# Six fp32 weight products of a two-layer graph network by Strassen's algorithm, in three phases of two weights

**Chip, cores, metric.** One core of one Trainium2 chip. The metric is the device time in microseconds (us) of one execution, taken on the chip; a "tile" is 128 tokens (two graphs of 64 nodes) on the partitions, a "pair" is two tiles, and there are 64 tiles.

## The reference

Everything is fp32. Cut to what matters:

```python
x: (128, 64, 768)   adj: (128, 64, 64) bool, symmetric, with the diagonal
# layer 0: 12 heads of 64
h    = einsum('bnd,ade->bane', x, W)                  # product 1, weight W
th   = tanh(h)
attn = th @ w_src + swap(th @ w_dst)                  # one number per node and head
attn = leaky_relu(attn, 0.2); attn = where(~adj, -999, attn)
f    = elu(softmax(attn) @ h + b)                     # mixing, 64 x 64 per graph and head
gate = sigmoid(x @ H_w.T + H_b)                       # product 2, weight H_w
x    = layernorm(x + gate * f + (1 - gate) * x)
# layer 1: 6 heads of 128
q, k, v = x @ Wq + bq, x @ Wk + bk, x @ Wv + bv       # products 3, 4, 5
p    = softmax(q @ k.T / sqrt(128) + where(adj, 0, -9e15))
x    = layernorm(x + (p @ v) @ Wf + bf)               # product 6
```

## The kernel before

All six weights lie in SBUF. A unit of layer 0 (half the heads of one tile) and the pieces of layer 1 for an earlier group of two tiles alternate in one stream, so that layer 0's work on VectorE, GpSimd and ScalarE lies beside the products of both layers. The parts that the change and the argument touch:

```python
def product(lhsT, w, half):                    # W, H_w, Wv, Wf: 128 tokens x 384 columns
    ps = psm.tile([P, HALF], F32, name="pm")
    for c in range(NC):                        # six matmuls of 128x384
        nc.tensor.matmul(ps, lhsT[:, c, :], w[:, c, halves(half)], start=(c == 0), stop=(c == NC - 1))
    return ps
...
for w, bias, name in ((wq_sb, bq_c, "qT"), (wk_sb, bk_c, "kT")):     # q, k: 256 tokens at a time
    for c in range(NC):
        nc.tensor.matmul(ps, w[:, c, cols], x1T[:, c, :, :], start=(c == 0), stop=(c == NC - 1))
...
def softmax(s, n):
    nc.vector.tensor_reduce(mx[:, :n], s, AX.X, ALU.max)
    nc.vector.tensor_tensor(s, s, mx[...].to_broadcast(...), ALU.subtract)
    nc.scalar.activation(s, s, AF.Exp)
    nc.vector.tensor_reduce(sm[:, :n], s, AX.X, ALU.add)
    nc.vector.reciprocal(rs[:, :n], sm[:, :n])
    nc.gpsimd.tensor_tensor(s, s, rs[...].to_broadcast(...), ALU.mult)
...
pieces = [(5, scores, (hd,)) for hd in range(HEADS)] + ...   # layer 1's pieces, each with its weight
# ---- the units of layer 0 in turn, each a step behind in parts, between pieces of layer 1 ----
```

## Time and profile before

| | before |
|---|---|
| time, median of 3 runs | 3660.8 us (3659.2 to 3661.57) |
| TensorE busy, instructions | 99%, 16228 |
| VectorE, GpSimd, ScalarE busy | 47%, 23%, 22% |
| mean granted clock of TensorE | 0.997 |

```profile
DVE  4545444544444454444544454444445444454442
```

### The profile page before, as it was taken

How to read it: one execution, taken by the hardware profiler on the slowest of the kernel's cores; microseconds unless marked ns; L12 is line 12 of the kernel's file. 1: busy time of each engine (PE TensorE's matmuls, PEld its weight loads, DVE VectorE, ACT ScalarE, POOL GpSimd, SP SyncE). 2: the span in 40 equal slices, each digit the busy share in tenths (PEclk: the TensorE clock that was granted, in tenths of full speed). 3: DMA queues.
4: the chain of work that ended last, by engine and by line, in shares of the span. 5: the costliest groups of instructions: out<-in, count | busy, mean ns of one | idle time of the engine just before them, and what ended most of it. 6: DMA issues, size and time to landing. Idle time of an engine off the chain costs nothing.

```text
span 3657.3 us, 40929 instructions
## 1 busy us (share of the span) xinstructions
PE 3605.6 (99%) x16228; PEld 2544.3 (70%) x16228; DVE 1721.5 (47%) x3821; ACT 810.4 (22%) x1925; POOL 852.3 (23%) x904
## 2 busy tenths in 40 slices
PE   6999999999999999999999999999999999999999
PEld 4776677766777666777667776677766677766776
DVE  4545444544444454444544454444445444454442
ACT  2222222222222222222222222222222222222221
POOL 2222212222222222122222222222222222222120
PEclk9999999999999999999999999999999999999999
DMA  6000000000000000000000000000000000000000
GB/s 204 1 18 18 18 10 9 18 18 18 9 10 18 18 18 10 9 18 18 18 18 9 9 18 18 18 9 10 18 18 18 9 10 18 18 18 14 5 5 18
DMA packets 44031, 69.25 MB, mean 19 GB/s; under 512 B 23104, under 2 KB 23104, under 8 KB 43840
## 3 DMA queue, kind: packets, MB, share of 16 engines
q1 hardware_dynamic: 43840, 66.64, 5.3%
q8 instruction: 128, 2.10, 0.2%
q14 instruction: 63, 0.52, 0.0%
HBM read 41.46 MB, written 25.17 MB: 18 GB/s over the span
## 4 chain that ended last, share of the span: by engine, by line
PE 88%; DVE 9%; POOL 1%; ACT 1%; SPq 0%; issue 0%; DMA 0%; POOLq 0%; ACTq 0%
PE pm L177 47%; PE pm L345 28%; PE pa L303 3%; PE pa L280 3%; PE pa L379 2%; PE pa L355 2%; PE pa L202 1%; DVE st L214 1%; POOL s L284 1%; DVE x L396 1%; PE pa L170 1%; DVE z L323 1%; DVE s L287 1%; DVE x L324 1%; DVE mx L185 1%; DVE s L283 1%
## 5 line engine op out<-in xcount | busy, mean ns | idle before, releaser
L345 PE MATMUL pm<-x1T,wq_sb 128*128 128x256 f32 x2304 | 560.3, 384 | 0.3 <-DVE x1T L171 0.3
L177 PE MATMUL pm<-w_sb,xT 128*128 128x384 f32 x1536 | 534.3, 494 | 13.9 <-DVE xT L171 13.4
L345 PE MATMUL pm<-x1T,wk_sb 128*128 128x256 f32 x2304 | 528.6, 379 | 0.0
L177 PE MATMUL pm<-wv_sb,x1T 128*128 128x384 f32 x1536 | 519.8, 488 | 0.0
L177 PE MATMUL pm<-wf_sb,cT 128*128 128x384 f32 x1536 | 517.9, 487 | 0.4 <-DVE cT L388 0.4
L177 PE MATMUL pm<-hw_sb,xT 128*128 128x384 f32 x1536 | 516.3, 486 | 0.0
L345 PEld LDWEIGHTS pm<-x1T,wk_sb 128*128 128x128 f32 x2304 | 437.8, 190 | 59.5
L345 PEld LDWEIGHTS pm<-x1T,wq_sb 128*128 128x128 f32 x2304 | 424.9, 190 | 62.6 <-DVE x1T L171 0.6
L177 PEld LDWEIGHTS pm<-hw_sb,xT 128*128 128x128 f32 x1536 | 291.8, 190 | 203.5
L177 PEld LDWEIGHTS pm<-w_sb,xT 128*128 128x128 f32 x1536 | 284.6, 190 | 199.8 <-DVE xT L171 21.1
L177 PEld LDWEIGHTS pm<-wf_sb,cT 128*128 128x128 f32 x1536 | 286.9, 190 | 187.3 <-DVE cT L388 0.7
L177 PEld LDWEIGHTS pm<-wv_sb,x1T 128*128 128x128 f32 x1536 | 284.3, 190 | 173.4
L358 DVE SCALAR_TENSOR_TENSOR s<-pa,fill 128x128 f32<-128x128 f32 x192 | 54.9, 286 | 661.7 <-PE pa L355 661.7
L250 POOL TENSOR_TENSOR tmp<-th,ws_bc 128x384 f32<-128x384 f32 x128 | 127.6, 997 | 903.7 <-ACT th L248 872.8
L194 POOL TENSOR_TENSOR s<-s,rs 128x384 f32<-128x384 f32 x192 | 177.2, 930 | 666.3 <-DVE rs L193 666.3
L284 POOL TENSOR_TENSOR s<-s,adjf 128x384 f32<-128x384 f32 x128 | 127.7, 998 | 717.1 <-DVE s L283 717.1
L209 ACT COPY pt<-pa 64x192 f32<-64x192 f32 x637 | 199.6, 313 | 428.0 <-PE pa L202 407.3
L303 PEld LDWEIGHTS pa<-h,pt 128*128 128x128 f32 x1536 | 195.4, 194 | 35.3 <-ACT pt L209 1.2
L246 DVE COPY h<-pm 128x384 f32<-128x384 f32 x128 | 71.3, 557 | 285.1 <-PE pm L177 285.1
L248 ACT ACTIVATE th<-pm 128x384 f32<-128x384 f32 x128 | 62.9, 491 | 592.6 <-DVE h L246 592.6
L303 PE MATMUL pa<-h,pt 128*128 128x64 f32 x1536 | 189.1, 273 | 0.1
L316 ACT ACTIVATE tmp<-tmp 128x384 f32<-128x384 f32 x128 | 66.9, 523 | 474.4 <-DVE tmp L315 474.4
(65 smaller groups left out, 3482.8 us busy)
## 6 DMA issues: line engine op xcount, KB each, us to landing
x<-in_x_dram SPq DMA_DIRECT2D x64, 384.0 KB, 2.9
out_dram<-x SPq DMA_DIRECT2D x64, 384.0 KB, 2.3
w_sb<-in_L_gnn_W_dram SPq DMA_DIRECT2D x6, 384.0 KB, 6.3
x<-in_L_gnn_H_w_dram SPq DMA_DIRECT2D x6, 384.0 KB, 7.2
wq_sb<-in_L_gnn_Wq_dram SPq DMA_DIRECT2D x6, 384.0 KB, 6.4
wk_sb<-in_L_gnn_Wk_dram SPq DMA_DIRECT2D x6, 384.0 KB, 7.8
wv_sb<-in_L_gnn_Wv_dram SPq DMA_DIRECT2D x6, 384.0 KB, 7.8
wf_sb<-in_L_gnn_Wf_dram SPq DMA_DIRECT2D x6, 384.0 KB, 7.8
```

Source lines behind the costliest of these rows:

```text
L177: nc.tensor.matmul(ps, lhsT[:, c, :], w[:, c, halves(half)], start=(c == 0), stop=(c == NC - 1))
L194: nc.gpsimd.tensor_tensor(s, s, rs[:, :n, None].to_broadcast([P, n, S]), ALU.mult)
L209: nc.any.tensor_copy(pt_v[own, :, h2, own], ps[h2 * S : (h2 + 1) * S, :, own])
L246: nc.vector.tensor_copy(h, ph)
L250: nc.gpsimd.tensor_tensor(tmp, th, ws_bc[:, hs], ALU.mult)
L280: nc.tensor.matmul(pd, same_graph, dg, start=True, stop=True)
L284: nc.gpsimd.tensor_tensor(s, s, adjf[:, i, None, :].to_broadcast([P, AH, S]), ALU.mult)
L303: nc.tensor.matmul(po[:, a, :], pts[0][:, a, :], h[:, a * E : (a + 1) * E], start=True, stop=True)
L316: nc.scalar.activation(e, e, AF.Exp)
L345: nc.tensor.matmul(ps, w[:, c, cols], x1T[:, c, :, :], start=(c == 0), stop=(c == NC - 1))
L355: nc.tensor.matmul(pc[own, i, :], qk[0][:, i, own], qk[1][:, i, own], start=True, stop=True)
L379: nc.tensor.matmul(pc[:, j, :], vs[i][:, hd * P : (hd + 1) * P], pts[1][:, hd, :], start=True, stop=True,)
```

## The change

The intent: TensorE is full, so take an eighth of its dense work away. Each product of two 2 x 2 block matrices needs 7 block products instead of 8 (Strassen's algorithm, in Winograd's form with few sums). The sums of the operands are formed by VectorE and GpSimd; the sums of the results are formed in PSUM, by reading an accumulator between two products that add to it. Seven combinations of a weight take 7/4 of its room; the changed kernel holds two weights at a time: phase 1 does W and H_w (layer 0) for all tiles in pairs, phase 2 does Wq and Wk on groups of eight tiles, phase 3 does Wv and Wf in pairs. Between the phases x1 (plain and transposed) and the probabilities go through DRAM. The diff, condensed to its core (lines joined and shortened; `...` marks what is left out):

```diff
+def block_products(mm, done):                 # 7 products in 3 PSUM accumulators A, B, D
+    s0: mm(A, P1, True)
+    s1: mm(B, P6, True);   done("p1", A)
+    s2: mm(D, P7, True);   done("r", B)       # r = B + P1, read before the next line adds to B
+    s3: mm(B, P5, False);  done("w", B)       # w = B + P1, again a read between two additions
+    s4: mm(A, P2, False);  done("c11", A); done("c22", D)
+    s5: mm(B, P3, False);  done("c12", B)
+    s6: mm(D, P4, False);  done("c21", D)
+def token_major(comb, w):                     # W, H_w, Wv, Wf: three matmuls of 128x384 a product
+    for c in range(CH):
+        nc.tensor.matmul(ps[:, :HALF], comb[i][:, c, :], w[:, i, c, :],
+            start=start and c == 0, stop=c == CH - 1, skip_group_check=not start)
-            xTs[t] = work.tile([P, NC, P], F32, name="xT")
-            transposed(xs[t], xTs[t])
+            nc.vector.tensor_sub(c[P7], c[P1], a21); nc.vector.tensor_add(c[P5], a21, c[P4])
+            nc.gpsimd.tensor_tensor(c[P6], c[P4], c[P7], ALU.subtract)
+            nc.gpsimd.tensor_tensor(c[P3], c[P2], c[P6], ALU.subtract)
 ...                                          # phase 1, step p of 33: 14 products of pair p, and
+            dense = h_pieces(p) + g_pieces(p)  # ahead of the numbered ones:
+            add(side, 9 + 2 * i, scores, 2 * p + i)        # pair p
+            add(side, 12, prep, p + 1)
+            add(side, 2 * i, spread, t, 0)                 # t: the tiles of pair p - 1
+            add(side, 2 * i + 1, probs, t)                 # leaky, mask, softmax
+            add(side, 5 + 3 * i, turned, t, 0)             # transposes of the probabilities
+            add(side, 7 + 3 * i, mixed, t, 0)
+            add(side, 8 + 3 * i, rest, t)                  # elu, gate, residual, layernorm
+            add(side, 14, x1_turned, t)                    # transposed result, to DRAM
 ...
+x1_d, x1T_d, pr_d = DRAM tiles                # phase 1 -> 2 and 3, 1 -> 2 and 3, 2 -> 3
```

Layer 0's operations now take all 12 heads at once (768 columns), and the mask is one addition of 0 or -1e30 instead of a product and a sum.

## The prediction

Its 0.4292 us for a 512-column instruction lies on the straight line through the two spacings that it measures (0.2158 us for 256 columns, 0.3225 for 384). Its 0.557 us for a VectorE operation of 384 columns is in its trace (L246). The 6 us that bring its second rival to 50 us a pair are an estimate that no run had shown.

> **What bounds the kernel now.** I read the page's busy shares and slices first, then the chain that ended last, then the groups of instructions, then TensorE and VectorE instruction by instruction in the timeline.
>
> ```profile
> PE 3605.6 (99%) x16228; PEld 2544.3 (70%) x16228; DVE 1721.5 (47%) x3821; ACT 810.4 (22%) x1925; POOL 852.3 (23%) x904
> ...
> PE   6999999999999999999999999999999999999999
> ...
> PE 88%; DVE 9%; POOL 1%; ACT 1%; SPq 0%; issue 0%; DMA 0%; POOLq 0%; ACTq 0%
> ```
>
> TensorE is full in every slice but the first, and 88% of the chain is TensorE. No other engine passes half. So the time is TensorE's instruction stream plus the start. What the stream consists of, from the groups:
>
> ```profile
> L345 PE MATMUL pm<-x1T,wq_sb 128*128 128x256 f32 x2304 | 560.3, 384 | 0.3 <-DVE x1T L171 0.3
> L177 PE MATMUL pm<-w_sb,xT 128*128 128x384 f32 x1536 | 534.3, 494 | 13.9 <-DVE xT L171 13.4
> ```
>
> There are two groups of the first kind (q, k) and four of the second. The mean of one (384, 494 ns) is not its price, as matmuls overlap. The price is the distance between starts in the timeline:
>
> ```profile
> 1822.99 2.75 PE L345 MATMUL pm<-x1T,wk_sb 128*128 128x256 f32 x12
> 1825.58 1.03 PE L345 MATMUL pm<-x1T,wq_sb 128*128 128x256 f32 x4
> ...
> 1889.63 4.03 PE L177 MATMUL pm<-w_sb,xT 128*128 128x384 f32 x12
> 1893.50 4.03 PE L177 MATMUL pm<-hw_sb,xT 128*128 128x384 f32 x12
> ```
>
> Twelve 384-column instructions take 1893.50 - 1889.63 = 3.87 us, 0.3225 each; twelve 256-column ones 2.59 us, 0.2158 each. Each fp32 matmul of the source is two such instructions (64 tiles x 12 products = 768, and the row says 1536). The six products are then 6144 x 0.3225 + 4608 x 0.2158 = 1981 + 994 = 2976 us. In the same way from the timeline, the small work: 1536 mixing matmuls (L303) at 0.107, 768 of L379 at 0.115, 1344 transposes at 0.109, 1536 of L355 at 0.048, 256 of L280 at 0.3225: 165 + 88 + 147 + 74 + 83 = 557 us. Together 3533 us. The rest of 3657 is the start (first product at 27.9 us), an end of some 8 us, and about 90 us lost where kinds alternate.
>
> [...] So I estimate 512 columns at 429.2 ns. [...] one such line lasts 0.558 us at the median and up to 1.236:
>
> ```profile
> L324 DVE SCALAR_TENSOR_TENSOR x<-x,z x128: 545/558/1236, 56.5 to 3560.0; 128x384 f32<-128x384 f32 x128
> ```
>
> **The change, part by part.**
>
> *Removed from TensorE.* Strassen takes 7 block products for 8. For a pair of tiles and one of the four token-major weights it is 7 x 3 = 21 matmuls for 24; for q and k, on groups of eight tiles, 63 of 512 columns per weight for 144 of 256. So 5376 instructions x 0.3225 = 1734 us, and 2 x 8 x 63 x 2 = 2016 x 0.4292 = 865 us. Sum 2599, a saving of 377 us. The counts of small matmuls stay. TensorE's own work becomes 3533 - 377 = 3156 us: per pair of tiles in phase 1, 84 x 0.3225 = 27.1 plus 11.7 small = 38.8 us; phase 2, 865 + 74 = 939 us in all; phase 3, 30.5 us per pair.
>
> *Added elsewhere.* Three accumulators serve a block of seven products, and TensorE waits twice per block for a read of the bank it will add to next (first r, then w, from the same bank), and once for c22. Each read has one product's time to happen: 3 x 2 x 0.3225 = 1.94 us, or 2.58 us in phase 2. In a free VectorE (0.56 us, 0.69 for 512 columns) it is hidden.
>
> *VectorE in phase 1.* From the instruction order of the changed kernel, per pair: 27 ops of 384 columns (operand sums 2, h 5, gate 8, spread 4, mixed 4, statistics 4) and 20 of 768 (four reductions for the scores, eight in the softmaxes and leaky part, eight in the residual), plus 1.5 us of small ones: 27 x 0.557 + 20 x 0.96 + 1.5 = 35.7 us beside 38.8 of TensorE. Back to back they start closer than they last:
>
> ```profile
> 1851.11 0.55 DVE L186 TENSOR_TENSOR s<-s,mx 128x384 f32<-128x384 f32 x1
> 1851.58 0.55 DVE L317 SCALAR_TENSOR_TENSOR z<-z,tmp 128x384 f32<-128x384 f32 x1
> 1852.05 0.22 DVE L228 TENSOR_SCALAR fill<-adjf 128x128 f32<-128x128 f32 x1
> ```
>
> 0.47 us apart instead of 0.56. So VectorE's load is some 33 us, yet in strict order with waits for GpSimd and ScalarE between. GpSimd's own load per pair is about 21 us, by these prices, doubled for 768 columns:
>
> ```profile
> L250 POOL TENSOR_TENSOR tmp<-th,ws_bc 128x384 f32<-128x384 f32 x128 | 127.6, 997 | 903.7 <-ACT th L248 872.8
> ...
> L365 POOL TENSOR_TENSOR x<-x,bf_bc 128x768 f32<-128x768 f32 x64 | 115.0, 1820 | 100.3 <-PE pa L170 100.3
> ```
>
> I then walked one pair by hand[...], in us from the first product of h, at 1.94 a product and the durations above. (1) r of h is read at 4.7; the spreads and the leaky part of the first tile end at 7.6; GpSimd adds its mask until 9.5; VectorE, in order, takes the max at 9.6, a spread, the subtraction and the second tile's leaky part, and so reads w at 13.0 to 13.6, when TensorE wanted that bank at 12.9: stall 0.8. (2) The first tile's sum follows exp at 14.5, its reciprocal stands behind the second tile's max, which waits for GpSimd until 15.0, so GpSimd divides from 16.2 to 18.1 and TensorE's transposes of the probabilities, wanted at 15.6, start at 18.2: stall 2.5. (3) r of the gate stands behind a score reduction that waits for GpSimd's product until 30.0: read at 32.5, wanted at 31.1: 1.5. (4) c22 of the gate stands behind the second tile's statistics and the wait for GpSimd's power: read at 42.5, wanted at 41.0: 1.5. (5) The turn of the second tile's result waits for its layernorm: 1.9. That is 8.2 us, 47 us per pair. The shorter distances of some 40 ops give back about 3. I take **44 us** a pair.
>
> *The three phases.* Start 25 us to the first product and 29 us for a first pair without side work; 31 x 44 = 1364; then a tail with no dense work, one latency chain of softmax, mixing, residual, layernorm and turn, with the second tile behind it: 36. Into phase 2: both weights are issued before the end, but three of the four operand loads stand behind the last store, 0.8 MB each, then three sums of 1536 columns at 1.76: 18. Phase 2: 939 and some 11 for stalls behind the softmaxes: 950. Into phase 3: weights come during k, the first pair's transposed rows must be loaded and summed on GpSimd: 10. Phase 3: 32 x 31 with alternation = 992, stalls of 0.7 a pair: 1015. End: layernorm and store, 10. Sum 25 + 29 + 1364 + 36 + 18 + 950 + 10 + 1015 + 10 = 3457, say **3460 us**. So of the 377 us, 200 arrive; roughly 160 go to stalls in phase 1 and the rest to the two hand-ons.
>
> **The rivals.** *TensorE stays the bound everywhere.* The code spreads its side work over the fourteen products, which speaks for it, as does VectorE's 47% before. Then a phase-1 pair costs about 40 us: 3457 - 31 x 4 = 3333. *VectorE becomes phase 1's bound[...].* [...] Then 50 us a pair: 3643, no gain. The single line above that stretched was hit in few of its 128 cases, which speaks against the full size. *DRAM traffic and small packets hold it up.* The page has 19 GB/s before; the change adds 25 MB six times over (x1 out and in, its transpose out and twice in, the probabilities out and in at half that each), 151 MB in 3.4 ms or 44 GB/s, while the first slice moved 204 GB/s. That is hidden except at the hand-ons; if those cost 60 us more, 3520. *The products stall in all phases* (each read a little late): 14 more stalls of 0.3 us in 32 pairs of phase 3 would be 130 us, 3590; VectorE is only some 12 us of 31 there, which speaks against it.
>
> **Range and chances.** The pair of phase 1 is the wide term: 41 to 48 us give 3364 to 3581; the hand-ons add 20 either way. I take 3350 to 3600. Faster than 3588 with 0.85, within 2% 0.12, slower 0.03.
>
> **What would show it right or wrong.** Right: 5376 matmuls of 128x384 at 0.32 us apart and 2016 of 128x512 at 0.43; TensorE idle in phase 1 put down to VectorE and GpSimd (accumulator reads, probabilities, turns) at about 5 us a pair; phase 1 ending near 1455 us; VectorE's busy digits at 7 or 8 in phase 1, 4 in phase 2 and 3 or 4 in phase 3; gaps of 50 and 10 us at the hand-ons. Wrong: a phase-1 period below 41 (the walk too pessimistic) or over 48[...]; a stretched 512-column instruction; phases 2 or 3 more than 3% over their TensorE work.

## The result, and the profile after

The changed kernel takes **3538.6 us** (median of 4 runs, 3536.2 to 3541.5), before 3660.2 us in the same rounds: ratio **0.967**, 95% interval 0.965 to 0.968. A ratio here is the mean time of one kernel's fast runs over that of the other's of the same rounds, so not quite the ratio of the medians.

The page of the kernel after: busy shares, slices, chain.

```profile
PE 3280.1 (93%) x12868; PEld 1935.3 (55%) x12868; DVE 1830.0 (52%) x3067; ACT 852.3 (24%) x1677; POOL 1287.8 (36%) x984
...
PE   8888988889889888859999999999899999999998
...
DVE  4777777777777777752444234433433333333333
...
PE 46%; DVE 25%; POOL 18%; ACT 5%; issue 4%; SPq 0%; DMA 0%; POOLq 0%; ACTq 0%; DVEq 0%
```

TensorE's busy time fell by 325 us and the span by 118. The slices show three phases: up to the 17th, VectorE stands at 7 and TensorE at 8 or 9; in the rest TensorE is full. And the chain of waits, which was 88% TensorE, is now only 46%. The same by stretch (columns: stretch, length, then busy us of TensorE, weight loads, VectorE, ScalarE and GpSimd, granted clock, DMA share, GB/s):

```profile
50.00:1450.00 1400.00, 1246.15 (x5235) 811.28 (x5234) 1008.59 (x1657) 528.86 (x1040) 655.68 (x416) 0.96 0.16 50
...
1560.00:2480.00 920.00, 909.00 (x3449) 420.02 (x3450) 339.57 (x439) 85.80 (x128) 42.83 (x30) 0.99 0.12 41
...
2560.00:3500.00 940.00, 919.67 (x3418) 576.17 (x3417) 335.41 (x750) 176.71 (x390) 455.27 (x444) 1.00 0.27 85
```

Phases 2 and 3 are TensorE-bound, as predicted. In phase 1 TensorE is idle 11% of the time. The instructions of TensorE in one pair of phase 1 (from the timeline; the wait before an instruction and what ended it stand in brackets):

```profile
818.27 2.17 PE L180 MATMUL pm<-w,comb 128*128 128x384 f32 x6 [0.25 <-DVE w L350]
822.98 0.87 PE L220 MATMUL pa<-ident,s 128*128 128x128 f32 x6 [2.54 <-POOL s L214]
...
838.18 3.43 PE L180 MATMUL pm<-w,comb 128*128 128x384 f32 x6 [2.02 <-DVE r L376]
841.40 1.94 PE L442 MATMUL pa<-h,pt 128*128 128x64 f32 x12
843.18 2.15 PE L180 MATMUL pm<-w,comb 128*128 128x384 f32 x6
...
855.61 0.88 PE L477 MATMUL pa<-ident,z 128*128 128x128 f32 x6 [0.49 <-ACT z L202]
```

L220 are the transposes of the probabilities, waiting for GpSimd's division; L180 with "r" is a product that waits for VectorE's read of the accumulator. After the second wait six products take 841.40 - 838.18 = 3.22 us instead of 1.94, because the granted clock was halved for a while (columns as in the table by stretch above):

```profile
839.02:842.43 3.41, 3.41 (x11) 2.20 (x9) 3.41 (x4) 0.00 (x0) 2.05 (x1) 0.50 0.00 0
842.43:869.74 27.31, 24.12 (x94) 14.59 (x93) 21.50 (x40) 10.27 (x16) 9.91 (x7) 1.00 0.27 87
```

The clock records of the trace have 27 such stretches of 3.41 us at half clock from 100 to 1400 us, one a pair, so a pair loses about 1.7 us of TensorE time to them. They do not follow every wait: after the first one above, at 823, the clock stayed at 1.00. The mean pair, from the starts of GpSimd's L403 between 200 and 1300 us (all "pair" figures below are taken so), takes 46.95 us, and TensorE waits 143 us in the 1300 us from 100 to 1400, which is 5.2 us a pair.

The hand-ons, on TensorE's timeline: the tail of phase 1 has two waits of over 10 us, phase 2 begins at 1566.67, and phase 3 waits for its first transposed rows from DRAM.

```profile
1523.29 1.54 PE L477 MATMUL pa<-ident,z 128*128 128x128 f32 x6 [10.80 <-ACT z L202]
...
1539.76 1.54 PE L220 MATMUL pa<-ident,s 128*128 128x128 f32 x6 [10.46 <-POOL s L214]
...
1566.67 4.13 PE L572 MATMUL pm<-a,w 128*128 128x512 f32 x6
...
2515.64 4.21 PE L180 MATMUL pm<-w,xT 128*128 128x384 f32 x6 [11.16 <-DMA xT<-x1T]
```

### The profile page after: what moved, and what is told of

Same layout as the page of the kernel before. It is cut to its first block, busy times and chain, and to the rows that moved or that the text cites. A ratio compares the mean times of both kernels' runs of the same rounds, so it can differ in the third digit from the quotient of the medians.

```text
span 3539.0 us, 34181 instructions
## 1 busy us (share of the span) xinstructions
PE 3280.1 (93%) x12868; PEld 1935.3 (55%) x12868; DVE 1830.0 (52%) x3067; ACT 852.3 (24%) x1677; POOL 1287.8 (36%) x984
## 4 chain that ended last, share of the span: by engine, by line
PE 46%; DVE 25%; POOL 18%; ACT 5%; issue 4%; SPq 0%; DMA 0%; POOLq 0%; ACTq 0%; DVEq 0%
PE pm L572 25%; PE pm L180 16%; POOL u L396 5%; POOL s L427 3%; ACT pt L227 3%; DVE st L194 3%; DVE z L463 2%; DVE z L458 2%; POOL s L214 2%; POOL rstd L199 2%; DVE mx L207 2%; DVE sd L397 2%; DVE s L426 2%; DVE z L459 2%; DVE z L462 2%
## 5 line engine op out<-in xcount | busy, mean ns | idle before, releaser
L180 PE MATMUL pm<-w,comb 128*128 128x384 f32 x2688 | 981.9, 510 | 50.8 <-DVE r L376 34.3
L180 PEld LDWEIGHTS pm<-w,comb 128*128 128x128 f32 x2688 | 511.3, 199 | 375.0 <-issue 64.5
L572 PE MATMUL pm<-o,w 128*128 128x512 f32 x1152 | 524.0, 598 | 0.0
L572 PE MATMUL pm<-a,w 128*128 128x512 f32 x864 | 389.2, 595 | 7.2 <-issue 7.2
L572 PEld LDWEIGHTS pm<-o,w 128*128 128x128 f32 x1152 | 215.8, 190 | 258.3 <-issue 254.1
L180 PE MATMUL pm<-w,so 128*128 128x384 f32 x768 | 271.7, 497 | 25.8 <-DVE r L723 20.3
L572 PEld LDWEIGHTS pm<-a,w 128*128 128x128 f32 x864 | 164.8, 191 | 214.5 <-issue 214.5
L180 PE MATMUL pm<-w,sc 128*128 128x384 f32 x768 | 263.6, 486 | 0.0
L180 PE MATMUL pm<-w,xT 128*128 128x384 f32 x576 | 203.7, 490 | 11.2 <-DMA xT<-x1T 11.2
L180 PEld LDWEIGHTS pm<-w,so 128*128 128x128 f32 x768 | 143.0, 193 | 121.0 <-DVE r L723 27.5
L180 PE MATMUL pm<-w,cT 128*128 128x384 f32 x576 | 201.3, 486 | 0.0
L180 PEld LDWEIGHTS pm<-w,sc 128*128 128x128 f32 x768 | 141.1, 190 | 85.6 <-DVE r L777 0.6
L403 POOL TENSOR_TENSOR dg<-eye,sd 128x768 f32<-128x768 f32 x64 | 113.5, 1773 | 131.5 <-DVE sd L397 130.3
```

The costliest lines, as they stand in the source:

```text
L180: nc.tensor.matmul(ps[:, :HALF], comb[i][:, c, :], w[:, i, c, :], start=start and c == 0, stop=c == CH - 1, skip_group_check=not start,)
L403: nc.gpsimd.tensor_tensor(dg, eye[:, None, :].to_broadcast([P, A, S]), sd[:, 1, :, None].to_broadcast([P, A, S]), ALU.mult,)
L572: nc.tensor.matmul(ps, w[:, i, c, j * P : (j + 1) * P], opers[g][i][:, c, :], start=start and c == 0, stop=c == CH - 1, skip_group_check=n ...
```

## The experiments

The question: 377 us of TensorE work were taken away and 122 us arrived. Where did the rest go, and what sets phase 1? Theory A was that the streams of VectorE and GpSimd set the pair and TensorE merely waits for them; its rivals were (B) that TensorE's own work counts in full with waits on top, and (C) that each wait comes from one instruction's place in its engine's stream and can be moved away. Each expectation says itself what its theories mean (B means something else in nomax_udve, and D comes in with nomax_split); 46.85 and 45.7 us in them are earlier readings of the pairs of the changed kernel and of nomax. All twelve kernels but the last give correct results, and a ratio is to the kernel before (3661 us) in the same rounds.

| run | us | ratio | pair, us | TensorE waits a pair, us | lost to the clock a pair, us |
|---|---|---|---|---|---|
| changed kernel | 3538.6 | 0.967 | 46.95 | 5.2 | 1.7 |
| plain_p1 | 3677.3 | 1.005 | 51.96 | 5.8 | 2.3 |
| plain_all | 3865.1 | 1.056 | 51.75 | 5.8 | 2.4 |
| repeat | 3616.3 | 0.988 | 49.42 | 5.9 | 1.7 |
| nomax | 3505.2 | 0.958 | 46.08 | 4.6 | 1.7 |
| defer | 3558.6 | 0.972 | 47.75 | 5.7 | 1.6 |
| turn | 3520.2 | 0.962 | 46.32 | 4.3 | 1.7 |
| turn_scores | 3559.8 | 0.973 | 47.83 | 4.5 | 3.4 |
| turn_scores_nomax | 3549.0 | 0.970 | 47.78 | 4.7 | 3.4 |
| nomax_split | 3503.1 | 0.957 | 46.08 | 4.6 | 1.7 |
| nomax_udve | 3516.3 | 0.961 | 46.75 | 5.1 | 2.3 |
| nomax_behind | 3516.6 | 0.960 | 46.90 | 5.0 | 2.3 |
| cut (wrong result) | 3523.2 | 0.962 | 47.06 | 4.9 | 2.6 |

The last but one column is the sum of TensorE's waits from 100 to 1400 us, times the pair, over 1300. It stays between 4.3 and 5.9. The last is half of the time for which the trace's clock records show half clock, brought to a pair in the same way. A pair is TensorE's own work (38.8 us; 42.7 in the plain kernels, 40.7 in repeat), plus these two, plus 0.5 to 1.7 us of the rest. This split adds up by construction and names no cause.

### What the phases cost, and what Strassen gives

The same three phases with the ordinary eight block products, first in phase 1 alone, then everywhere:

```diff
-        w_w = weight(load_w)                 # seven combinations
+        w_w = weight_plain(load_w)           # four blocks
-            return block_products(token_major(combs[p], w_w), done)
+            return block_plain(token_plain(combs[p], w_w), done)   # c11 = P1 P1 + P2 P2, and so on
```

> Phase 1 with plain block products (8 for 7), phases 2 and 3 left with Strassen. Theory A: a pair of phase 1 (46.85 us) is set by VectorE and GpSimd taking turns in order, and TensorE only waits; then 3.87 us more TensorE work per pair cost nothing, and the 7 VectorE and 2 GpSimd operations that go make the pair shorter: 44 to 45 us (TensorE's own 42.7 plus alternation is the floor), some 3470 us in all. Theory B: TensorE's work plus stalls that have other causes sets it: 46.85 + 3.87 = 50.7 us a pair, 3660 us.

> The three phases without Strassen anywhere. Phases 2 and 3 are bound by TensorE and each grow by its work: 288 x 0.4292 = 124 us and 32 x 3.87 = 124 us. Theory A: 248 us over the run with a plain phase 1, some 3720 us, so that phases as such cost 60 us against the kernel before. Theory B: 3660 + 248 = 3905 us.

Measured: 3677.3 and 3865.1 us (the runs of plain_all spread from 3850 to 3876). Both times theory B's forecast (3660, 3905) was far nearer than A's (3470, 3720). So the rearrangement into phases by itself *costs* 204 us (3865 - 3661), and Strassen's algorithm on top of it gives 326 (3865 - 3539). The trace of plain_all, against that of the changed kernel, shows where the 326 come from. Phase 2 begins 1694.86 - 1566.67 = 128 us earlier (TensorE's work saved in phase 1: 32 pairs x 12 instructions x 0.3225 = 124). Phase 2 up to its last instruction on TensorE is 1056 - 938 = 118 us shorter (of 124). Phase 3 is 1107 - 1023 = 84 us shorter (of 124): its pair falls from 34.30 to 31.37 us, 2.93 of the 3.87 saved, because each pair of the changed kernel waits once for an accumulator read. The list of waits has 0.68 us for it, the starts on the timeline 0.94: three transposes start at 2707.71 and the products after the next six at 2710.92, 3.21 us for 0.33 + 1.94 of work.

The loss lies in phase 1. A pair of plain_all takes 51.75 us, while TensorE's work in it is 96 x 0.3225 + 11.7 = 42.7: 9 us x 31 = 281 us lost, more than the 204, as the kernel before had losses too (some 90 us where kinds alternate, by the prediction's estimate; in its trace the eight instructions of q after one group of layer 1's scores, L355, take 1.83 us, 1821.16 to 1822.99, instead of 1.73). The kernel before did layer 0's same work with nearly no waits, beside the products of both layers; the phases put all of it beside layer 0's products alone. How busy VectorE is does not explain the loss: plain_all's page has VectorE at 5 tenths in phase 1, hardly above the 4 or 5 of the kernel before. Another reading, which no run separates from the first, is that the new kernel issues the steps of one tile's chain (scores, softmax, mixing, layernorm) with too few products between them.

Theory A in the form "VectorE's amount of work sets phase 1" had plain_p1 faster, as the plain products need fewer VectorE operations. VectorE's busy share did fall (58% from 100 to 1400 us, against 72% in the changed kernel), and the run was 139 us slower, so that form falls. The run does not show more than that, since its order changed too: in plain_p1 the chain of waits (explained below) runs on TensorE from 811.22 to 826.7, through 28 product instructions and some small matmuls, where the chain of the changed kernel meets no product.

### Is TensorE's work on the path? The first product twice

```diff
             mm(a["A"], P1, True)
+            if again:                        # in phase 1, first product of W only
+                mm(a["A"], P1, True)
```

> The changed kernel with the first product of h computed twice for each pair (it starts its accumulator anew, so the result is the same): 1.94 us more TensorE work per pair and nothing more for VectorE. If phase 1's pair were set by the other engines, under 15 us more in all; if TensorE's work adds to its waits: 60 us more (32 x 1.94), 3600 us, less what the longer stream hides of the waits.

Measured: 3616.3 us, and 2.47 us a pair for 1.94 us of TensorE work added. I read this at first as proof that TensorE's work counts in full. The chain of waits (below) does not bear that out. In the changed kernel the first tile's score product on GpSimd starts 4.2 us after the transposes of the probabilities (822.98 to 827.14). In this run it starts 6.9 us after them (857.04 to 863.89), behind the second tile's exponential, sum and division. These came late, as VectorE's stream now had the second tile's leaky part after the first tile's sum, where the changed kernel has it before. So the edit, which adds to TensorE's stream alone in the source, changed the order of the other engines' streams too, and that difference of 2.7 us is as large as the slowdown. The run does not show what it was meant to show.

### Shortening the softmax

The logits of layer 0 are bounded by the weights (at most 2 x 64 x 0.304 = 39 in size), so the maximum is left out (the result of this run is correct):

```diff
-            softmax(s, A)
+            softmax(s, A, shift=False)       # no maximum, no subtraction; layer 0 only
```

> Strassen everywhere; layer 0's softmax without the subtraction of the maximum (its logits are bounded by the weights, so the result should still agree). Two 768-column VectorE operations per tile go, and with them the wait of VectorE for GpSimd's mask. Theory A: 3.6 us of the chain go per pair: 43 us, 3425 us. Theory B: only the stall of 2.5 us before the transposes of the probabilities shrinks, and TensorE's 38.8 plus the rest stays: 45 us or more, 3480 us.

Measured: 3505.2 us, 33 us less, so B's forecast (45 us a pair or more, 3480 us) was nearer than A's (43 us, 3425 us): the pair falls by 0.87 us although 3.8 us of VectorE work a pair are gone. TensorE's wait for the probabilities fell from 2.5 to 1.15 us, but the wait for r of the gate grew to 3.1. (Waits of TensorE in this run, 100 to 1400 us: us in total, times, longest.)

```profile
PE pm L180 <- DVE r L377: 86.1, 28, 3.1
PE pa L221 <- POOL s L215: 32.2, 28, 1.2
```

The other way to relieve the division is to do it after the mixing. That takes one 768-column operation a tile from GpSimd and gives VectorE two more of 384 columns:

```diff
-            softmax(s, A)
+            rss[t] = softmax0(s, A)          # keeps 1/sum instead of dividing
+            nc.vector.tensor_tensor(zv, po, rss[t][...].to_broadcast([P, 6, E]), ALU.mult)
```

> Strassen everywhere; layer 0's probabilities are divided by their sum only after the mixing (VectorE multiplies by the reciprocal as it reads PSUM, then adds the bias: four more 384-column operations a pair), and GpSimd's two divisions of 1.5 to 2.0 us go. Theory A with GpSimd's turn as the part that counts: the 2.5 us stall goes, the four operations give back 1.9 at most: 44.5 to 46 us, 3450 to 3510 us. If VectorE's throughput alone counted: 48.5 us a pair, 3590 us.

Measured: 3558.6 us, 20 us more, between the two forecasts: the wait for the division is gone, and five others stand in its place: for three of VectorE's reads (1.2 to 1.4 us a pair each), for the layernorm (1.0) and for the exponential (0.7).

### Moving what waits

Later places in TensorE's stream for the transposes of the probabilities, and for the scores. In one place of the changed kernel's trace the work behind a waiting instruction did not pass it: VectorE had read the accumulator of h's last product by 822.06 (L358) and TensorE was idle from 820.44 to 822.98, yet this product started at 823.69, after the transposes that waited for the division.

```diff
-                    add(side, 5 + 3 * i, turned, t, 0)
+                    add(side, 7 + 2 * i, turned, t, 0)       # turn; mixed and rest follow it
-                    add(side, 9 + 2 * i, scores, 2 * p + i)
+                    add(side, 10 + 3 * i, scores, 2 * p + i) # turn_scores, and with nomax
```

> Strassen everywhere; in phase 1 the transposes of the probabilities come two products later in the source for the first tile and one later for the second, with mixing and residual behind them. Theory C: TensorE waits in phase 1 because its in-order stream places too little work between a chain's start (the spread) and its end (the transposes), whatever the load of VectorE. Then the 2.5 us wait for GpSimd's division goes: 44.3 us or less a pair, 3460 us or less. If VectorE's load set the pair, nothing: 3540 us.

> The same, and the scores of both tiles issued one and two products later, which puts the gate's read of r ahead of all four score reductions in VectorE's order. Theory C: the wait for r (1.1 us on average, 2.0 at most, and the clock's drop after it) goes as well: 43 us a pair, 3420 us. If VectorE's load set the pair: 3540 us.

> The same without the maximum in layer 0's softmax. Theory C: little waiting is left, 41 to 42 us a pair (38.8 TensorE work, 1 for alternation, 1 to 2 waits), 3370 to 3400 us. If VectorE's load set the pair: 3.6 us less than 46.85, so 3430 us.

Measured: 3520.2, 3559.8 and 3549.0 us, so theory C's forecasts (3460, 3420, 3370 to 3400) all failed. In turn the wait for the division is gone from the list, and waits for w of h (2.4 us) and before the transposes of x (1.3) have taken its place; in turn_scores the same waits alternate from pair to pair; in the third, one wait of 4.2 us for VectorE's read of the mixing is left. The sum stays at 4.3 to 4.7 us. The last two wait less than the changed kernel and are slower all the same: their granted clock in phase 1 is 0.93, against 0.96, and the clock takes 3.4 us a pair instead of 1.7. The pairs differ by less than that (0.8 to 0.9 us).

### Moving one wait in VectorE's stream

In the trace of nomax, VectorE's read of r stands behind the score reductions of the second tile, which wait for GpSimd (VectorE and TensorE, from the timeline):

```profile
819.73 0.95 DVE L398 TENSOR_REDUCE sd<-u 128x12 f32<-128x768 f32 x1 [0.82 <-POOL u L397]
...
821.47 0.55 DVE L377 TENSOR_TENSOR r<-pm,p 128x384 f32<-128x384 f32 x1
...
822.07 3.62 PE L180 MATMUL pm<-w,comb 128*128 128x384 f32 x6 [3.07 <-DVE r L377]
```

VectorE kept to this order although the read could have come sooner: TensorE was idle for 3.07 us before 822.07, so r's product had ended by 819.00, and VectorE, idle until 819.73, still took the reductions first and the read at 821.47. Three ways to undo it:

```diff
 nomax_split:   reductions in a function of their own, one product later in the source
 nomax_udve:    -nc.gpsimd.tensor_tensor(u[:, i], th, w, ALU.mult)
                +(nc.vector if i else nc.gpsimd).tensor_tensor(u[:, i], th, w, ALU.mult)
 nomax_behind:  +an ordering edge (no wait): second tile's reductions issue after the read of r
```

> Layer 0 without the softmax's maximum, as before, and now the two score reductions of a tile stand one product later in VectorE's queue than the GpSimd products that they read. In the trace of the run without the maximum, VectorE waits 2.03 and 0.82 us for GpSimd in these reductions while the read of r of the gate stands behind them, and TensorE loses 3.07 us there in each pair, and after it some 1.5 us at a lower clock. Theory C (the order of waits within VectorE's in-order stream sets the stalls): that wait falls under 0.7 us a pair, the lower clock after it goes, the pair takes 41 to 43 us instead of 45.7, and the kernel 3380 to 3430 us. Rival D (some chain of latencies as long as the pair sets the period, and a wait removed here comes back elsewhere): 3480 to 3520 us, the sum of TensorE's waits in phase 1 about what it was (some 4.5 us a pair), under other lines.

> Layer 0 without the softmax's maximum, and the second of the two score multiplications of a tile on VectorE (0.95 us) instead of GpSimd (1.81 us). VectorE then has 1.9 us a pair more to do and GpSimd 3.6 us less. Theory C: what counts is that VectorE no longer waits for GpSimd's second product ahead of r of the gate; the wait of 3.07 us falls to about 1, the kernel to 3410 to 3460 us. Rival B (a busy VectorE is what costs, be it ordered as it may): more VectorE work, so 3505 to 3550 us. Rival D: 3480 to 3520 us with the waits elsewhere.

> The run that moved the score reductions in the source showed the same order of instructions in VectorE's stream and so tested nothing[...]. Here an ordering edge (issue order only, no wait) puts the two score reductions of the second tile of a pair behind the read of r of the gate; the built kernel's VectorE stream shows r of the gate ahead of them, which it was not before. Nothing else is changed against the run without the maximum: the same work on every engine. Theory C (order of the waits within VectorE's in-order stream): TensorE's wait for r of the gate, 3.07 us a pair, falls under 0.7, and the 1.5 us at a lower clock after it go as well; a pair takes 41 to 42.5 us instead of 45.7 and the kernel 3370 to 3420 us. Rival D (a chain of latencies as long as the pair): 3480 to 3520 us, TensorE's waits in phase 1 in sum unchanged (some 4.5 us a pair) but under other lines.

Measured: 3503.1, 3516.3 and 3516.6 us. **nomax_split** tested nothing: the scheduler restored VectorE's order exactly, and the trace shows the same 3.07 us wait. **nomax_behind** did put r ahead, and the wait for r vanished. But a wait of 3.25 us for the division stands in its place (it was 1.15 in nomax):

```profile
PE pa L221 <- POOL s L215: 91.0, 28, 3.3
```

nomax_udve ended the same way (90.9 us in 28 waits for the division, and 1.6 us a pair for the layernorm). Theory C's expectation of 3370 to 3420 us failed by 100 us, and rival D's number (3480 to 3520) came true. But the traces show why the wait grew, and the reason is not D's. The expectation's "Nothing else is changed" was wrong: the scheduler also exchanged two operations in GpSimd's stream. In nomax GpSimd divides the first tile (L215) and then adds the second tile's mask (L428):

```profile
801.45 2.04 POOL L215 TENSOR_TENSOR s<-s,rs 128x768 f32<-128x768 f32 x1 [2.60 <-DVE rs L214]
803.46 1.81 POOL L428 TENSOR_TENSOR s<-s,fill 128x768 f32<-128x768 f32 x1
```

In nomax_behind the mask (L444) comes first:

```profile
804.76 1.80 POOL L444 TENSOR_TENSOR s<-s,fill 128x768 f32<-128x768 f32 x1 [2.87 <-DVE rs L214]
806.52 1.47 POOL L215 TENSOR_TENSOR s<-s,rs 128x768 f32<-128x768 f32 x1
808.05 0.87 PE L221 MATMUL pa<-ident,s 128*128 128x128 f32 x6 [3.25 <-POOL s L215]
```

The wait is 2.1 us longer with a mask of 1.8 us ahead of the division, and nomax_udve has the same order (mask at 806.01, division at 807.77), as the changed kernel has (817.80 and 820.88, in the chain below). So these two runs took one wait away and put another in by a second exchange. They do not decide between C and D. A run with r ahead and the division still first was not made.

### Removing TensorE's largest wait

The last run lets TensorE transpose a constant tile in place of the probabilities. The result is wrong (relative error 0.58). All other engines still do the whole softmax. VectorE's stream holds the same instructions with a few neighbours swapped, and on GpSimd the first tile's first score product now stands ahead of the second tile's division.

```diff
-            probs_transposed(ss[t][:, half * 6 : (half + 1) * 6, :], pts[...])
+            probs_transposed(ws_bc.rearrange("p (a m) -> p a m", m=S)[:, half * 6 : (half + 1) * 6, :], pts[...])
```

> Wrong result on purpose: in layer 0 TensorE transposes a tile that never changes in place of the probabilities, so that it never waits for GpSimd's division; VectorE, GpSimd and ScalarE still work out the whole softmax, and the built kernel's VectorE stream has the same instructions in nearly the same order (a few neighbours swapped). It takes away the largest of TensorE's waits in phase 1, 2.54 us a pair. Theory C (each wait is its own, by its place in the streams): the sum of TensorE's waits falls from 5.3 to about 3 us a pair and some of the clock loss goes: 43 to 44 us a pair, 3440 to 3465 us. Rival D (the other engines' streams have no slack, so what TensorE does not wait for here it waits for at the next accumulator read): 3505 to 3540 us, the sum still 4.5 to 5.5 us a pair, now put down to VectorE's reads.

Measured: 3523.2 us, 15 us less, but the mean pair takes 47.06 us (46.95 with the wait). Phase 2 begins 19 us earlier (1547.84): the last dense product of phase 1 ends 10 us earlier, from the start and the first pairs and from the last pair, and the tail after it is 9 us shorter. The 2.5 us came back at two accumulator reads (waits of TensorE, 100 to 1400 us):

```profile
PE pm L180 <- DVE r L376: 92.7, 28, 3.3
PE pm L180 <- DVE h L358: 38.5, 28, 1.4
```

The mean hides two kinds of pair (here from one copy of ScalarE's L352 to the next):

```profile
766.46:812.37 45.91, 41.20 (x178) 27.05 (x177) 34.20 (x58) 17.68 (x35) 22.02 (x15) 0.96 0.16 52
812.37:860.20 47.83, 42.96 (x178) 28.65 (x177) 34.30 (x57) 17.68 (x35) 22.02 (x15) 0.93 0.15 50
```

The waits are alike in both (4.7 and 4.9 us). Pairs with one stretch at half clock take 45.9 to 46.2 us; those with two, more than half of the pairs from 390 us on, take 47.8. Each steady pair of the changed kernel has one stretch and takes 46.8 to 47.2. So at equal clock, taking a wait of 2.5 us away gave some 0.9 us, and in the mean a lower clock took that back.

That the wait came back at other places agrees with D, and with the chain of waits of the *changed* kernel. Followed through one pair of phase 1 it reads (start, us, what; cut to its larger pieces):

```profile
808.76 0.87 PE pa L477 x6
809.63 1.31 PE pa L416 x4
...
812.66 1.82 POOL s L427
...
817.80 1.82 POOL s L427
...
820.88 2.06 POOL s L214
...
822.98 0.56 PE pa L220 x3
...
827.14 3.59 POOL u L396 x2
...
837.66 0.47 DVE r L376
```

From 810.9 to 823.0 the chain is the softmax of both tiles, passed between VectorE and GpSimd; then the copies of the transposes on ScalarE, the tanh, score products on GpSimd with their reductions, the read of r, and the residual on VectorE until the next turn at 855. TensorE holds 2.7 of these 47 us, all of it small matmuls. From the turn (L477) to the end of the read of r it is 808.76 to 838.13, 29.4 us; in cut, without the wait that lies in this half of the pair, it is 803.14 to 832.15, 29.0. Summed over the chain from 100 to 1300 us: VectorE 50%, GpSimd 29%, ScalarE 9%, TensorE 6%, issue 5%. So by this chain TensorE's products in the changed kernel's phase 1 lie beside the path, and its 5 us of waits are the slack that is left. What survives of theory A is this chain of latencies in a fixed order, not an amount of work, and it is read from the trace, not isolated by a run: VectorE itself is busy only 72% of phase 1 (1009 of 1400 us).

The same view of the other runs shows why their single edits gained so little: the path goes over to TensorE (26% of it in nomax, 28% in cut, 37% in nomax_behind, 41% in turn_scores; 21% in plain_p1). A part of that is the lower clock: in cut, the three pieces after the wait for r take 8.8 us on the chain (832.20 to 841.02) for 5.2 us of work at the full clock.

**What stays open.** Why the sum of the waits stays between 4.3 and 5.9 us in every variant is not settled. Each edit also changed the order in which the scheduler issued the rest, so no run isolates one place in a stream. Theory B is not refuted either: if TensorE's products lay beside the path with 5 us of slack, more of them should have cost little at first, but the runs that added TensorE work took longer by all of it and more (repeat 2.47 us a pair for 1.94, plain_p1 5.0 for 3.87). And why the clock is halved once in some pairs and twice in others was not tested. A version with all streams ordered by hand could tell, and was not tried. The fastest correct versions that ran are nomax_split and nomax, which have the same order: 3503 and 3505 us, 0.957 and 0.958 of the kernel before.

## Why the prediction was right, and where it was not

The prediction was 3460 us with a range of 3350 to 3600; measured 3538.6, faster by 3.3%. Its parts in turn:

- **TensorE's work** was right. In phase 3 twelve 384-column instructions take 3.87 us, as before; in phase 2 eighteen of 512 columns take 7.72 us (1598.65 to 1606.37), 0.429 each, as estimated.
- **Reading a partial sum between two products that add to it** works: the results are correct, and in phase 2, where a product of 512 columns takes 2.58 us, no wait for such a read is listed at all.
- **The pair of phase 1 is the term that was too small**: 44 us predicted, 46.95 measured, 2.95 x 31 = 91 us, more than the whole error of 79. The loads that went into it were right: VectorE 33 us a pair (1008.59 x 46.95 / 1400 = 33.8 measured), GpSimd 21 (22.0). The stalls that the walk found were 8.2 us, less 3 given back by shorter distances; measured are 5.2. Their places were half right: division 2.5 (predicted 2.5), r of the gate 1.1 (1.5), w of h 0.25 (0.8), the turn of x1 0.5 (1.9), c22 of the gate none (1.5), and 0.7 before the transposes of x, which the walk did not have. That their sum came out at 5.2, as forecast, is partly luck. What the sum lacked is the 46.95 - 38.8 - 5.2 = 3.0 us beside them: matmuls at half clock in one stretch of 3.41 us a pair (1.7 us; in the pair shown 1.28 in the six products and 0.5 in the twelve small matmuls after them) and, for the other 1.3, in part two things that the timeline shows. The list counts a wait from the modelled end of the last matmul, which lies 0.16 to 0.24 us behind the distance of starts: over the four waits of the pair shown, 0.7 us. And the six products after a mixing take 1.99 us (843.18 to 845.17) instead of 1.94. The prediction counted changes between kinds of matmul in phase 3 and for the kernel before, but not in phase 1, and had no term for the clock.
- **The picture behind that term** was wrong in a deeper way, which its size hides: it adds stalls to TensorE's work. The chain of the changed kernel is a path through the other engines, 94% of it off TensorE, and the run cut agrees with it in part. The walk did follow that path, so the number came out near; its reading "TensorE plus stalls" would have promised 2.5 us a pair for removing the division's wait, and that gave some 0.9 at equal clock and nothing in the mean.
- **Rivals.** "TensorE stays the bound everywhere" (3333) is refuted by phase 1. "VectorE becomes phase 1's bound" had the right engines and the wrong size. Two groups of VectorE operations last longer than their like, and no run isolates why. In the pair shown, L463 took 1.75 us (from 841.11, overlapping GpSimd's L403, 840.00 to 842.05) and one L458 1.68 (from 835.99, overlapping L396, 835.04 to 836.85); their shortest cases took 0.95 and 0.94. L462, which overlaps the same L403 (from 839.78), took 0.94 and never more than 0.96. The numbers after the first bar are busy us and mean ns of one:

```profile
L463 DVE SCALAR_TENSOR_TENSOR z<-x,z 128x768 f32<-128x768 f32 x64 | 95.9, 1499 | 0.0
...
L462 DVE SCALAR_TENSOR_TENSOR z<-gt,z 128x768 f32<-128x768 f32 x64 | 60.6, 947 | 0.0
```

  That is (1499 - 947) x 2 = 1.1 us a pair for L463, and (1301 - 947) x 2 = 0.7 for the only other group that stretches as much, against the 6 us (50 - 44) of this rival. "DRAM holds it up" (3520): at 62 GB/s in the mean, TensorE's waits for a DMA are 6.5 us at the start and 11.2 at the second hand-on, and at the first VectorE's sums of the operands wait 9.4 us for one. "Stalls in all phases" (3590): phase 3 has one of 0.68 us a pair, as the sum had assumed (0.7).
- **Hand-ons.** The tail of phase 1 from the last dense product (1512.5) to the steady start of phase 2 (1578.0) took 65.5 us, predicted 36 + 18 = 54. Two weights' sums for phase 2 come ahead of the last tiles' layernorm (VectorE: L129 at 1513.93 and L128 at 1517.07, L201 at 1519.62; GpSimd: L131 at 1515.35, L199 at 1517.92), and the small matmuls of the tail run at about half clock (0.57 granted from 1512.5 to 1578.0; six transposes 1.54 us instead of 0.82). From phase 2 to 3: 11 us (10). Start and first pair: the second pair's work begins at about 53 us (54), by luck: the first product starts at 7.0 us, not 25, and the first pair, which waits 5.1 us for the sums of H_w's weight, takes the rest.
- **Phase 2** was 926.5 us, 23.5 less than the 950 predicted: 32 score matmuls of 64 columns start 1.08 us apart, 0.034 each, where the walk used 0.048 from the kernel before, and the 11 us of stalls behind the softmaxes did not come. Phase 3 was 1015 us as predicted, with 31.37 us a pair. The sum of all these differences is 91 + 11.5 - 23.5 = 79 us.

## What to carry to other kernels

Before taking work off a full engine, ask what will lie beside it afterwards: here the new arrangement, with one layer's side work beside that layer's products alone, cost 204 us, and the algorithm's 326 us had to pay that first. Where a chain of short operations passes between engines, as here, neither busy shares nor the list of waits told what a wait was worth: follow the chain that ended last, test by removing a wait alone, and compare pairs at equal clock. And check the built order of instructions on every engine before an experiment on order is read: a scheduler can undo the edit, or move the rest.

## What else the traces show

- In phase 1 of the changed kernel no wait of a steady pair is longer than 2.6 us, and still the granted clock fell to 0.50 for 3.41 us once a pair, within 1 us of the end of the gap of 2.02 us at 838 or of that of 2.54 us at 870, though not after the one of 2.54 us at 823. Mean clock of phase 1: 0.96.
- fp32 instructions of TensorE start 0.2158, 0.3225 and 0.429 us apart for 256, 384 and 512 columns, and the trace has two of them for each matmul of the source.
- In phase 1 of the changed kernel VectorE is busy 1009 of 1400 us (weight loads 811) and holds half of the chain. But taking 3.8 us a pair off VectorE (nomax) gave 0.87, and plain_p1, with VectorE at 58%, was slower: the share did not tell what its work is worth.
- On VectorE 384-column operations that last 0.55 us start 0.47 us apart (821.51 and 821.98 in the changed kernel), and 768-column ones that last 0.95 us start 0.87 apart (838.05 and 838.92).
